# Side products of TensorE in four groups of 32 columns, and row maxima without a sum, in a two-layer graph attention kernel

## The chip, the cores and the metric

The kernel runs on one core of a Trainium2 chip. A core has TensorE (matrix products, into PSUM), VectorE, ScalarE, GpSimd and a synchronising engine that issues transfers; each runs its own list of instructions in order and waits for the others through semaphores. The metric is the device time of one execution in microseconds: 10420.47 us in the median of three runs of the kernel before (10419.83 to 10420.89).

## The reference

N = 3327 nodes with D = 128 features, and an adjacency matrix `adj` of zeros and ones with ones on its diagonal. Layer 0 is a graph attention, layer 1 eight "heads" of attention over a reshaped projection; each is added to its input and normalised by row.

```python
# layer 0
H = X @ W.T + b
s = H @ a_s
r = H @ a_r
e = leaky_relu(A * s + A * r.T, negative_slope=0.2)
att = softmax(where(A > 0, e, NEG), axis=1)
x = layernorm(x + att @ H)
# layer 1: h = 8, d = 128, n = 3327
q = (x @ Wq.T).reshape(d, n, h); k, v likewise
a = einsum('dnh,dmh->dnm', q, k) * d ** -0.5 + adj + adj
out = einsum('dnm,dmh->dnh', softmax(a, axis=2), v)
x = layernorm(x + out.reshape(n, h * d) @ Wo.T)
```

The reshape turns each of the 128 features into an attention of its own over all 3327 nodes with vectors of eight numbers. So layer 1 has 128 times 3327 x 3327 scores, each with an exponential, and this is nearly all of the work.

## The kernel before

**Main loop.** Features go in 32 groups of four. A group's columns go in 7 blocks of 476. The 3327 rows go in 26 tiles (`NT`), a "stretch" being three of them. A block has 26 rounds, and a round makes four score products (L135, one tile of scores `scb` for each two features, contraction over 32 rows, so that the four features use the four groups of 32 rows of TensorE's array) and then the four products with v of a tile of some rounds earlier (L800, `av`, one feature for each group of 32 columns of the array). Between them, a tile's scores take one of two ways. In a third of the tiles ScalarE makes the exponential from PSUM (L994) and GpSimd multiplies by a factor made of the adjacency (L995). In the others VectorE adds the adjacency from PSUM (L997) and ScalarE makes the exponential in place (L830). In the first two rounds of a stretch half the scores go one way and half the other; in the third all go VectorE's way. The PSUM tiles of ScalarE's way are one buffer, those of VectorE's way two, and the scores of a round wait for the buffer they write to be read. LAG = 4 is the number of rounds by which the products with v come later.

**Side work.** Layer 0 for tiles 1 to 25, the projections to q, k and v, and the last product with Wo are cut into small pieces and strewn over the rounds by `work_tensor` (pieces for TensorE, after the scores and ahead of the products with v) and `work` (pieces for VectorE and GpSimd, after the round's own additions). The function `lane` says which rounds have room for a piece: the middle one of each three, and the rounds at a block's ends. `finish_to` makes the pieces that are due before a group can start, one after the other. All of TensorE's pieces write to one PSUM bank, `bank`, which has one buffer. The order on every engine is that in which the program is written (`tc.manual_schedule`).

The pieces that matter here:

- `weigh` (L284) makes on VectorE, for a tile of 128 rows of layer 0 and one chunk of 128 columns, the maximum of a row `trow` (the same for all partitions) and a number of each partition, `er`. It asks also for the sum of what it makes, which is written to `spare` and read by nothing. The masks (`mask`, L295) are multiplied in on GpSimd. `count` (L304) is VectorE's count of zeros and ones in the adjacency.
- `product` (L311) multiplies 26 such chunks with `hsb` and sums them in the bank: 128 rows of weights, 128 columns, 129 numbers for each.
- `project` in `layer0` (L365) makes 128 columns of q, k or v from a tile of `x1T`; `halves` (L374, L377) or `values` (L396) empties the bank.
- `project` in `result` (L479) multiplies with Wo, eight pieces for a tile of 128 rows.

`load_row` (L257) brings `trow` from `td` in DRAM. The tile 0 of layer 0 is made ahead of the main loop, with `side=False`.

Of the kernel before, what the change touches and what calls it, by code (L numbers as in the profile page):

```python
# [8 lines left out]
F32 = mybir.dt.float32  # L9
# [4 lines left out]
ALU = mybir.AluOpType  # L14
# [3 lines left out]
P = 128  # L18
# [16 lines left out]
def _ap(t, offset, dims):  # L35
    return bass.AP(tensor=t.tensor, offset=t.offset + offset, ap=[list(d) for d in dims])
# [11 lines left out]
def kernel(  # L48
# [27 lines left out]
    nc = tc.nc  # L76
    N, D = x.shape
    H = wqT.shape[1]
    assert D == P
    NT = -(-N // P)  # L80
# [10 lines left out]
    FP = N // NT  # L91
    kr = [FP + (i < N - FP * NT) for i in range(NT)]
    assert FP == P - 1
    REST = N - FP * NT
# [7 lines left out]
    dram = ctx.enter_context(tc.tile_pool(name="dram", bufs=1, space=bass.MemoryType.DRAM))  # L102
# [6 lines left out]

    oT = dram.tile([H1, G], F32, name="oT")  # L110
    x1d = dram.tile([N, D], F32, name="x1d")
    td = dram.tile([1, N], F32, name="td")

# [12 lines left out]
    wo = const.tile([P, H, D], F32, name="wo")  # L128
# [15 lines left out]
    def special():  # L144
        with ExitStack() as sx, tc.manual_schedule(engines=ALL):
            keep = sx.enter_context(tc.tile_pool(name="sx_keep", bufs=1))
            bg2 = sx.enter_context(tc.tile_pool(name="sx_bg2", bufs=2))
            bga = sx.enter_context(tc.tile_pool(name="sx_bga", bufs=3))
            bgw = sx.enter_context(tc.tile_pool(name="sx_bgw", bufs=2))
            bg1 = sx.enter_context(tc.tile_pool(name="sx_bg1", bufs=1))  # L150
            bps = sx.enter_context(tc.tile_pool(name="sx_ps", bufs=1, space=bass.MemoryType.PSUM))

            CW = -(-NT // 3)
            CH = [(i, min(i + CW, NT)) for i in range(0, NT, CW)]

            wq = keep.tile([P, H * D], F32, name="wq")
# [13 lines left out]
            one_row = keep.tile([1, P], F32, name="one_row")  # L170
            nc.vector.memset(one_row, 1.0)
            nrm = keep.tile([1, 4], F32, name="nrm")

            spare = keep.tile([P, 1], F32, name="spare")
            ones = keep.tile([P, 1], F32, name="ones")
            nc.vector.memset(ones, 1.0)

            def bank(shape=(P, 512)):
                return bps.tile(list(shape), F32, tag="bank", name="bank")

            def rsqrt(s, v, r):

                def parts():
                    w = s["root"]
                    return w[:r, 0:1], w[:r, 1:2], w[:r, 2:3]

                def first():
                    s["root"] = bg1.tile([P, 4], F32, name="root")  # L190
                    nc.vector.tensor_scalar(parts()[0], v(), EPS, None, op0=ALU.add)

                def shift():
                    ve, y, z = parts()
                    nc.vector.tensor_scalar(z.bitcast(I32), ve.bitcast(I32), 1, None, op0=ALU.logical_shift_right)

                def guess():
                    ve, y, z = parts()
                    nc.vector.tensor_scalar(
                        y.bitcast(I32), z.bitcast(I32), -1.0, 1597463007.0, op0=ALU.mult, op1=ALU.add  # L200
                    )

                def error():
                    ve, y, z = parts()
                    nc.vector.tensor_scalar(z, y, ve, y, op0=ALU.mult, op1=ALU.mult)

                def factor():
                    ve, y, z = parts()
                    nc.vector.tensor_scalar(z, z, -0.5, 1.5, op0=ALU.mult, op1=ALU.add)

                def better():
                    ve, y, z = parts()
                    nc.vector.tensor_scalar(y, y, z, None, op0=ALU.mult)

                return [first, shift, guess] + [error, factor, better] * 3

            def together(*fs):
                def run():
# [22 lines left out]
            def layer0(t, side=True, trow=None, bank=bank):  # L241
# [4 lines left out]
                r = rows[t]  # L246
                s = {"a": {}, "w": {}}
# [5 lines left out]
                        nc.sync.dma_start(s["x"][p0:p1], x[t * P + p0 : t * P + p1, :])  # L253

                def load_row():
                    s["t"] = bg2.tile([P, P], F32, name="trow")
                    nc.sync.dma_start(s["t"][:, :r], _ap(td, t * P, [[0, P], [1, r]]))  # L257

                def load_adj(n):
                    i0, i1 = CH[n]  # L260
# [15 lines left out]
                def weigh(n, c0, c1):  # L276
                    i0 = CH[n][0]
                    if c0 == i0:
                        s["w"][n] = bgw.tile([P, CW, P], F32, name="w")
                    for i in range(c0, c1):  # L280
                        w, e = s["w"][n][:, i - i0, :r], er[:, i : i + 1]
                        if side:

                            nc.vector.tensor_scalar(  # L284
                                w, s["t"][:, :r], e, None, op0=ALU.max, op1=ALU.add, accum_out=spare[:, 0:1]
                            )
                        else:
                            nc.vector.scalar_tensor_tensor(
                                w, s["b"][:, :r], e, s["a"][n][:, i - i0, :r], op0=ALU.max, op1=ALU.mult
                            )  # L290
# [17 lines left out]
                def product(i):  # L308
                    if i == 0:
                        s["p"] = bank()  # L310
                    nc.tensor.matmul(  # L311
                        s["p"][:r, : D + 1],
                        s["w"][i // CW][: kr[i], i % CW, :r],
                        hsb[: kr[i], i, :],
                        start=(i == 0),
                        stop=(i == NT - 1),
                    )
# [43 lines left out]
                QW = 128 if side else 512  # L361

                def project(w, c):
                    s["b"] = bank()
                    nc.tensor.matmul(s["b"][:r, :QW], s["xT"][:, :r], w[:, c : c + QW], start=True, stop=True)  # L365

                def halves(dst, c, scale):
                    if c % 512 == 0:
# [53 lines left out]
                for n, (i0, i1) in enumerate(CH):  # L422

                    aside.append(("n", ("P", q0 + n - 2, 0)))
                    for c0 in range(i0, i1, 3):
                        c1 = min(c0 + 3, i1)
# [6 lines left out]
                    c = [("d", lambda n=n, h=h, k=k: count(n, h, k)) for h in range(3) for k in range(2)]  # L433
# [6 lines left out]
            def result(t):  # L440

                r = rows[t]
                s = {}
# [32 lines left out]
                def project(h):  # L476
                    if h == 0:
                        s["b"] = bank()
                    nc.tensor.matmul(  # L479
                        s["b"][:r, :D], s["ot"][:, h, :r], wo[:, h, :], start=(h == 0), stop=(h == H - 1)  # L480
                    )

                def finish():
# [32 lines left out]
            def judge():  # L516

                s = {}
                lim = 2.718281828 ** ((1 - ALPHA) * SAFE0)

                def load():
                    s["t"] = bg1.tile([P, NT], F32, name="jt")
                    nc.gpsimd.memset(s["t"], 1.0)
                    nc.sync.dma_start(s["t"][:FP, :], td[0, : FP * NT].rearrange("(p i) -> p i", i=NT))
                    nc.sync.dma_start(s["t"][FP:P, :REST], td[:, FP * NT :])

                def square(n, w, i):
                    u = bg1.tile([P, H, P], F32, name="ot")[:, :4, :].rearrange("p a b -> p (a b)")
# [73 lines left out]
            with ExitStack() as st:  # L602
# [6 lines left out]
                xT = pro.tile([P, P * NT], F32, name="xT")  # L609
# [39 lines left out]
                for b, (n0, _) in enumerate(blocks):  # L649
                    pr = pps.tile([P, 512], F32, tag="mm", name="pr")  # L650
                    nc.tensor.matmul(pr[:1, :WB], ascol, hT[:, n0 : n0 + WB], start=True, stop=True)
                    nc.scalar.activation(trs[b], pr[:1, :WB], AF.Exp, scale=ALPHA - 1.0)
                    nc.scalar.dma_start(td[:, n0 : n0 + WB], trs[b])

                for n, i0 in enumerate(range(0, NT, 3)):
                    pb = pps.tile([P, 512], F32, tag="mm", name="pb")[:, : 3 * (D + 1)].rearrange(
# [51 lines left out]
            for m, st_ in enumerate(stretch):  # L708
                starts[len(rounds)] = m
                if len(st_) > 1:  # L710
                    i = st_[0]
# [242 lines left out]
            for g in range(NG):  # L954
                k4, v4, _ = group
                for b in range(NBLK):
                    s = Block()
# [440 lines left out]
```

## Time and profile before

| what | value |
|---|---|
| time, median of 3 | 10420.47 us |
| span of the profiled execution | 10418.4 us |
| TensorE matmuls busy | 10195.1 us (98%) |
| ScalarE busy | 10088.8 us (97%) |
| VectorE busy | 9410.9 us (90%) |
| GpSimd busy | 9223.5 us (89%) |
| L311, matmul records and their busy time | 1300, 318.4 us |
| L365 (three groups) | 1200, 293.9 us |
| L479 | 416, 101.5 us |
| L284, maxima | 650 operations, with their accumulator readings 220.9 us |

The profile counts an engine as busy while an instruction of it is in work. Matmuls overlap and their ends are modelled, so that a busy TensorE is not one at its peak; there the distance from one start to the next says more than the length. An fp32 product is two records of a matmul and two of a weight load. "Idle before <-" tells how long an engine stood still before the instructions of a group and what released it. The chain that ended last is the way back from the last instruction through whatever released each one. Line numbers are those of the kernel before; in the kernel after, the products of L311 and L365 stand in the helpers `by_columns` (L224) and `whole` (L182), those of L479 in `by_columns` too.

### The profile page before, as it was taken

How to read it: one execution, taken by the hardware profiler on the slowest of the kernel's cores; microseconds unless marked ns; L12 is line 12 of the kernel's file. 1: busy time of each engine (PE TensorE's matmuls, PEld its weight loads, DVE VectorE, ACT ScalarE, POOL GpSimd, SP SyncE). 2: the span in 40 equal slices, each digit the busy share in tenths (PEclk: the TensorE clock that was granted, in tenths of full speed). 3: DMA queues.
4: the chain of work that ended last, by engine and by line, in shares of the span. 5: the costliest groups of instructions: out<-in, count | busy, mean ns of one | idle time of the engine just before them, and what ended most of it. 6: DMA issues, size and time to landing. Idle time of an engine off the chain costs nothing.

```text
span 10418.4 us, 195134 instructions
## 1 busy us (share of the span) xinstructions
PE 10195.1 (98%) x73245; PEld 3823.1 (37%) x73245; DVE 9410.9 (90%) x12247; ACT 10088.8 (97%) x8311; POOL 9223.5 (89%) x4395
## 2 busy tenths in 40 slices
PE   7999999999999999999999999999999999999998
PEld 3333333333333333333333333333333333333333
DVE  6999999999989999989999999999999899998887
ACT  6999999999999999999999999999999999999998
POOL 6988898889888899888898888888888888898887
PEclk8999999999999999999999999999999999999999
DMA  6655555555555555555555555555555555545554
GB/s 173 199 172 163 168 167 170 169 167 162 172 163 163 170 161 167 173 164 163 163 166 172 167 173 162 154 171 171 167 170 163 158 171 170 171 147 170 162 157 125
DMA packets 1176730, 1728.90 MB, mean 166 GB/s; under 512 B 121853, under 2 KB 1164382, under 8 KB 1171548
## 3 DMA queue, kind: packets, MB, share of 16 engines
q1 hardware_dynamic: 1174410, 1714.80, 55.5%
q8 instruction: 576, 9.44, 0.4%
q14 instruction: 383, 3.13, 0.1%
q10 hardware_dynamic: 1361, 1.53, 0.1%
HBM read 1611.92 MB, written 103.95 MB: 165 GB/s over the span
## 4 chain that ended last, share of the span: by engine, by line
PE 84%; ACT 8%; DVE 4%; issue 1%; DMA 1%; POOL 1%; SPq 0%; DVEq 0%; ACTq 0%; POOLq 0%
PE av L800 44%; PE scb L135 34%; ACT e L994 5%; ACT e L830 3%; PE bank L311 3%; DVE e L997 2%; PE bank L365 2%; POOL e L995 1%; PE bank L479 1%; DVE o L809 1%; DMA at<-in_adjT_dram 0%; PE bank L460 0%; DVE ot L469 0%; DMA k4b<-kT 0%; DVE lo L377 0%
## 5 line engine op out<-in xcount | busy, mean ns | idle before, releaser
L995 POOL TENSOR_TENSOR e<-e,at 128x952 f32<-128x952 f32 x4032 | 8966.3, 2234 | 1078.4 <-ACT e L994 903.2
L997 DVE TENSOR_TENSOR e<-scb,at 128x952 f32<-128x952 f32 (+1 forms) x7616 | 8417.6, 1144 | 857.5 <-PE scb L135 639.1
L830 ACT ACTIVATE e<-e 128x1904 f32<-128x1904 f32 (+2 forms) x4256 | 6875.3, 1621 | 17.5 <-DVE e L997 16.4
L800 PE MATMUL av<-e,v4b 128*32 128x476 f32 x46592 | 5905.4, 575 | 37.6 <-DVE o L809 30.7
L135 PE MATMUL scb<-q4b,k4b 32*128 32x476 f32 (+1 forms) x23296 | 4339.0, 592 | 124.5 <-ACT e L994 62.3
L135 PEld LDWEIGHTS scb<-q4b,k4b 32*128 32x128 f32 (+1 forms) x23296 | 2378.4, 296 | 4925.1 <-issue 1936.8
L994 ACT ACTIVATE e<-scb 128x952 f32<-128x952 f32 x4032 | 3871.4, 960 | 228.9 <-PE scb L135 133.7
L800 PEld LDWEIGHTS av<-e,v4b 128*32 128x32 f32 x46592 | 948.3, 108 | 1223.1 <-issue 770.1
L311 PE MATMUL bank<-hsb,w 128*128 128x129 f32 (+2 forms) x1300 | 318.4, 327 | 0.0
L311 PEld LDWEIGHTS bank<-hsb,w 128*128 128x128 f32 (+2 forms) x1300 | 193.7, 188 | 148.2 <-issue 147.8
L304 DVE TENSOR_SCALAR_CACHE_REDUCE dump<-a 128x384 bf16<-128x384 f32 (+2 forms) x468 | 247.3, 528 | 0.6
L284 DVE TENSOR_SCALAR_CACHE_REDUCE w<-trow,er 128x128 f32<-128x128 f32 (+1 forms) x650 | 220.9, 340 | 20.6 <-DMA trow<-td 12.6
L295 POOL TENSOR_TENSOR w<-w,a 128x384 f32<-128x384 f32 (+3 forms) x225 | 221.8, 986 | 0.1
L809 DVE COPY o<-av 128x476 f32<-128x476 f32 x224 | 145.9, 651 | 27.6 <-PE av L800 6.8
L377 DVE SCALAR_TENSOR_TENSOR lo<-bank,hi 128x128 fp32r<-128x128 f32 (+1 forms) x400 | 116.6, 291 | 13.8
L374 DVE TENSOR_SCALAR hi<-bank 128x128 fp32r<-128x128 f32 (+1 forms) x400 | 112.3, 281 | 0.0
L365 PE MATMUL bank<-wv,x1T 128*128 128x128 f32 (+1 forms) x400 | 98.5, 328 | 4.1 <-DVE vb L396 4.0
L479 PE MATMUL bank<-wo,ot 128*128 128x128 f32 (+1 forms) x416 | 101.5, 330 | 0.4 <-DVE ot L469 0.4
L365 PE MATMUL bank<-wk,x1T 128*128 128x128 f32 (+1 forms) x400 | 97.7, 326 | 3.7 <-DVE lo L377 2.5
L365 PE MATMUL bank<-wq,x1T 128*128 128x128 f32 (+1 forms) x400 | 97.7, 326 | 3.2 <-DVE lo L377 2.5
L479 PEld LDWEIGHTS bank<-wo,ot 128*128 128x128 f32 (+1 forms) x416 | 63.0, 193 | 46.1 <-issue 45.5
L365 PEld LDWEIGHTS bank<-wv,x1T 128*128 128x128 f32 (+1 forms) x400 | 60.0, 189 | 50.8 <-issue 40.4
(111 smaller groups left out, 820.1 us busy)
## 6 DMA issues: line engine op xcount, KB each, us to landing
at<-in_adjT_dram SPq DMA_DIRECT2D x1736, 476.0 KB
at<-ftd SPq DMA_DIRECT2D x1953, 238.0 KB
q4b<-qT SPq DMA_DIRECT2D x1788, 29.8 KB
k4b<-kT SPq DMA_DIRECT2D x126, 415.9 KB
at<-in_adjT_dram SPq DMA_DIRECT2D x217, 208.2 KB
at<-in_adjT_dram SPq DMA_DIRECT2D x56, 714.0 KB
a<-in_adjT_dram SPq DMA_DIRECT2D x50, 504.0 KB
ftd<-at SPq DMA_DIRECT2D x63, 238.0 KB
```

What stands on the lines that cost most here:

```text
L135: nc.tensor.matmul(dst, k4[32 * j : 32 * j + H4, i::NT], q4[32 * j : 32 * j + H4, :nb], start=True, stop=stop,)
L295: nc.gpsimd.tensor_tensor(w, w, s["a"][n][:, c0 - i0 : c1 - i0, :r], op=ALU.mult)
L304: nc.vector.tensor_scalar(z, a, float(k), None, op0=ALU.is_equal, op1=ALU.add, accum_out=even[:, t, at : at + 1])
L311: nc.tensor.matmul(s["p"][:r, : D + 1], s["w"][i // CW][: kr[i], i % CW, :r], hsb[: kr[i], i, :], start=(i == 0), stop=(i == NT - 1),)
L365: nc.tensor.matmul(s["b"][:r, :QW], s["xT"][:, :r], w[:, c : c + QW], start=True, stop=True)
L479: nc.tensor.matmul(s["b"][:r, :D], s["ot"][:, h, :r], wo[:, h, :], start=(h == 0), stop=(h == H - 1))
L800: nc.tensor.matmul(s.av[32 * j : 32 * j + 32, :], s.v4[:r, j, i * H1 : i * H1 + 32], e[:r, j, :], start=(s.left == NT - 1), stop=(s.left = ...
L809: nc.vector.tensor_copy(o4, s.av)
L830: nc.scalar.activation(e, e, AF.Exp, scale=2.0)
L994: nc.scalar.activation(eh, z[:r, :, :WB], AF.Exp, scale=2.0)
L995: nc.gpsimd.tensor_tensor(eh, eh, ah, op=ALU.mult)
L997: nc.vector.tensor_tensor(eh, z[:r, :, :WB], ah, op=ALU.add)
```

## The change

The first part concerns TensorE. The side pieces of L311, L365 and L479 were each one product over the whole array of 128 columns. They become four products of 32 columns each, every one to its own 32 partitions of the bank, which is the form of the products with v that come after them. The numbers computed are the same. The second part concerns `weigh`: the sum and `spare` are gone. The row is laid out as three pieces of 43 numbers with one empty place after each, and the result is written as one run of 129. For this the tile `w` has rows of 129 numbers, `td` is longer by two, and `load_row` brings 129 numbers of which the last is not used (the two past the end of `td` are written with ones).

```diff
-    td = dram.tile([1, N], F32, name="td")
+    td = dram.tile([1, NT * P + 1], F32, name="td")
...
+            T3 = P // 3 + 1
...
-            spare = keep.tile([P, 1], F32, name="spare")
...
+            def whole(dst, w, mov, r, **kw):
+                nc.tensor.matmul(dst[:r], w[:, :r], mov, **kw)
...
+            def by_columns(dst, w, mov, r, **kw):
+
+                for c0 in range(0, r, 32):
+                    c1 = min(c0 + 32, r)
+                    nc.tensor.matmul(dst[c0:c1], w[:, c0:c1], mov, **kw)
...
                 def load_row():
-                    s["t"] = bg2.tile([P, P], F32, name="trow")
-                    nc.sync.dma_start(s["t"][:, :r], _ap(td, t * P, [[0, P], [1, r]]))
+
+                    s["t"] = bg2.tile([P, 3, T3 + 1], F32, name="trow")
+                    nc.sync.dma_start(s["t"][:, :, :T3], _ap(td, t * P, [[0, P], [T3, 3], [1, T3]]))
...
-                        s["w"][n] = bgw.tile([P, CW, P], F32, name="w")
+                        s["w"][n] = bgw.tile([P, CW, 3 * T3], F32, name="w")
...
                         if side:
 
-                            nc.vector.tensor_scalar(
-                                w, s["t"][:, :r], e, None, op0=ALU.max, op1=ALU.add, accum_out=spare[:, 0:1]
-                            )
+                            w = s["w"][n][:, i - i0, :].rearrange("p (a b) -> p a b", b=T3)
+                            nc.vector.tensor_scalar(w, s["t"][:, :, :T3], e, None, op0=ALU.max)
...
-                    nc.tensor.matmul(
-                        s["p"][:r, : D + 1],
-                        s["w"][i // CW][: kr[i], i % CW, :r],
+                    (by_columns if side else whole)(
+                        s["p"][:, : D + 1],
+                        s["w"][i // CW][: kr[i], i % CW, :],
                         hsb[: kr[i], i, :],
+                        r,
...
-                    nc.tensor.matmul(s["b"][:r, :QW], s["xT"][:, :r], w[:, c : c + QW], start=True, stop=True)
+                    (by_columns if side else whole)(
+                        s["b"][:, :QW], s["xT"], w[:, c : c + QW], r, start=True, stop=True
+                    )
...
-                    nc.tensor.matmul(
-                        s["b"][:r, :D], s["ot"][:, h, :r], wo[:, h, :], start=(h == 0), stop=(h == H - 1)
+                    by_columns(
+                        s["b"][:, :D], s["ot"][:, h, :], wo[:, h, :], r, start=(h == 0), stop=(h == H - 1)
                     )
...
-                    nc.sync.dma_start(s["t"][FP:P, :REST], td[:, FP * NT :])
+                    nc.sync.dma_start(s["t"][FP:P, :REST], td[:, FP * NT : N])
...
+                nc.scalar.dma_start(td[:, N:], one_row[:, : NT * P + 1 - N])
```

## The prediction

> **What bounds the kernel now.** I read the busy shares first, then the chain that ended last, then the costliest groups, and then single stretches.
>
> ```profile
> PE 10195.1 (98%) x73245; PEld 3823.1 (37%) x73245; DVE 9410.9 (90%) x12247; ACT 10088.8 (97%) x8311; POOL 9223.5 (89%) x4395
> PE 84%; ACT 8%; DVE 4%; issue 1%; DMA 1%; POOL 1%; SPq 0%; DVEq 0%; ACTq 0%; POOLq 0%
> L284 DVE TENSOR_SCALAR_CACHE_REDUCE w<-trow,er 128x128 f32<-128x128 f32 (+1 forms) x650 | 220.9, 340 | 20.6 <-DMA trow<-td 12.6
> L311 PE MATMUL bank<-hsb,w 128*128 128x129 f32 (+2 forms) x1300 | 318.4, 327 | 0.0
> L365 PE MATMUL bank<-wv,x1T 128*128 128x128 f32 (+1 forms) x400 | 98.5, 328 | 4.1 <-DVE vb L396 4.0
> L479 PE MATMUL bank<-wo,ot 128*128 128x128 f32 (+1 forms) x416 | 101.5, 330 | 0.4 <-DVE ot L469 0.4
> ```
>
> TensorE and ScalarE are both nearly full, so a gain on one soon meets the other. The chain runs through TensorE for 84%; the reader should see that the side pieces (L311, L365, L479) are few beside 46592 products with v, but stand in that chain. Each product is two matmul records because fp32 is run as two. TensorE's instructions in one stretch of three rounds:
>
> ```profile
> 5000.10 0.60 PE L135 MATMUL scb<-q4b,k4b 32*128 32x476 f32 x4
> 5000.63 0.49 PE L311 MATMUL bank<-hsb,w 128*128 128x129 f32 x2
> 5001.05 1.00 PE L800 MATMUL av<-e,v4b 128*32 128x476 f32 x8
> 5001.98 0.60 PE L135 MATMUL scb<-q4b,k4b 32*128 32x476 f32 x4
> 5002.52 1.01 PE L800 MATMUL av<-e,v4b 128*32 128x476 f32 x8
> 5003.45 1.04 PE L135 MATMUL scb<-q4b,k4b 32*128 32x476 f32 x4
> 5004.42 1.00 PE L800 MATMUL av<-e,v4b 128*32 128x476 f32 x8
> 5005.36 0.60 PE L135 MATMUL scb<-q4b,k4b 32*128 32x476 f32 x4
> ```
>
> Start to start is what counts here. Scores to the next product take 0.53 us, products with v 0.93, and the side product 5000.63 to 5001.05 = 0.42. The third round's scores take 1.04 instead of 0.60: taken one by one, its second pair starts 0.445 us after the first, 53 ns after VectorE's addition (L997) that frees their PSUM tile. That addition itself had waited for TensorE:
>
> ```profile
> 5002.69 3.26 DVE L997 TENSOR_TENSOR e<-scb,at 128x952 f32<-128x952 f32 x3 [0.30 <-PE scb L135]
> ```
>
> So a loop of TensorE and VectorE sets 5.26 us, and the side product is inside it. Where there is none, ScalarE runs without a gap:
>
> ```profile
> 10221.19 1.79 ACT L830 ACTIVATE e<-e 128x1904 f32<-128x1904 f32 x1
> 10222.88 0.96 ACT L994 ACTIVATE e<-scb 128x952 f32<-128x952 f32 x1
> 10223.72 1.80 ACT L830 ACTIVATE e<-e 128x1904 f32<-128x1904 f32 x1
> 10225.44 0.97 ACT L994 ACTIVATE e<-scb 128x952 f32<-128x952 f32 x1
> 10226.30 1.78 ACT L830 ACTIVATE e<-e 128x1904 f32<-128x1904 f32 x1
> ```
>
> From 10221.19 to 10226.30 are 5.1 us for the same four exponentials; the median of all such stretches is 5.068 without a side product and 5.259 with one. Whole blocks of 26 rounds (without, and with nine):
>
> ```profile
> 10209.26:10253.52 44.26, 42.64 (x312) 14.97 (x313) 38.19 (x36) 44.26 (x38) 40.07 (x19) 1.00 0.51 153
> 1267.07:1313.38 46.31, 45.84 (x335) 17.31 (x332) 40.59 (x48) 44.89 (x38) 40.85 (x20) 1.00 0.56 171
> ```
>
> ScalarE (fourth number after the length) is busy 44.26 of 44.26 in the first, 44.89 of 46.31 in the second. The difference is 2.05 us for nine products, 0.228 each, though each occupies TensorE for 0.42: the rest hides under ScalarE already.
>
> [...] the four column groups of a product with v start within 20 ns, and their second set starts 0.425 us after the first. [...] 0.512 from the second set to the next scores, of which 0.397 is streaming. [...] the product's second load starts 108 ns after the first, its second matmul 108 ns after that. [...]
>
> **The side pieces, part by part.** Lines 311, 365 and 479 of the side work are 650 + 600 + 208 = 1458 products. Each becomes four of 32 columns in the mode of the products with v that follow.
>
> Now: first load 0.107, second load beside the first matmul, second matmul 0.107, then 0.096 until the next load may start: 0.418. Then the products with v pay a first load of 0.425 - 0.397 = 0.027 that nothing hides. Together 0.445. After: a first load of 0.027, two sets that stream [...](0.1075 each, by the measure that 476 columns take 0.397), and no change of mode behind them; the next loads lie beside the second set, as the products' second loads do now. That is 0.242. If the load of each following set were not hidden, 0.027 twice, 0.296. The saving is between 0.15 and 0.20 us; I take 0.20, because the second set of the products with v shows a hidden load, and keep 0.15 for the range.
>
> How much of it reaches the end? In the middle of a block a product costs 5.259 - 5.068 = 0.19 over ScalarE's floor. With 0.20 less, TensorE's loop is 5.06, level with ScalarE. Two waits are in between. The second scores of the third-kind round can't start before VectorE's addition of the round before ends, 1.885 us after that round's start, which is when they start now; but the first pair goes ahead by 0.2, the addition that waited 0.30 for it follows, and that one starts the loop again. VectorE must then be free: its side operation between the two additions may last up to about 0.6. The counting (L304) takes 0.47 + 0.08, two halves (L374, L377) 0.6, two maxima 2 x 0.38 = 0.76 now. So the maxima would have become the bound there, and the second part of the change matters only through this.
>
> A fit of the 223 blocks' times to the products in them gives 0.178 us for each of 998 in the middle rounds and 0.242 for each of 452 at a block's ends: 178 + 109 = 287 us, the most that products can give back; hence no less than about 10133. I count 0.17 of the 0.178 in the middle (two bounds that are level disturb each other): 170 us. At the ends half of the projections wait for VectorE to empty the one bank (at 1265.71 a product waits 0.45 for L377), so an earlier start is lost there; I count 0.12: 54 us. Sum 224 us.
>
> **The maxima.** The operation loses its sum and the reading of the accumulator (83 ns, 650 times; 262 ns from one start to that reading, 119 from the reading to the next maximum, so 381). A plain one with a pointer scalar takes 214 ns at one element (L213); 129 elements[...] add 134: 348, less the 83 ns by which successive operations overlap, 265. Saved 116 x 650 = 75 us of VectorE, almost all of it beside other work. By itself I give it 0: stretches with two maxima have a median of 5.265 and 5.260 against 5.257 to 5.260 with other side work. The source is three rows of 43 in rows of 44, the destination one run of 129[...]. Rows of the masking operation (L295) now start every 129 elements: at most a few ns in 225 operations. The row loads bring 384 pieces of 172 bytes for 128 of 512, 25 times, a stage ahead of use; one small store at the start goes on ScalarE's queue, under 1 us.
>
> Added waits: TensorE gets 45 more instructions that only wait, each 51 ns, for its own earlier work[...].
>
> **The rivals.**
> 1. ScalarE or VectorE takes over sooner: only 0.08 reaches the end per product: 1458 x 0.08 = 117, so 10303. For it: ScalarE has 0.19 us per stretch to give and TensorE's loop then stands on it. Against: stretches without a product do reach 5.068 with all its waits.
> 2. Instruction issue: a product is now 16 instructions for 4. [...] Against: two waiting instructions of TensorE are 111 ns apart with nothing between, and 125 with a load and a matmul between.
> 3. [...] 2.23 us multiplications fill GpSimd for 89%, so VectorE would wait about 1 us per pair in 325 places: +290 - 224 = about 10490, slower. [...]
> 4. Nothing gained: the four groups take as long as the one: 10420.
>
> **How the numbers follow.** The forecast 0.68, rival 1 0.15, rival 2 0.04, rival 3 0.08, no change 0.05. Time: 10420 - 224 = about 10196. Low end: all 287 us, 10135. High end: rival 1 with its spread, 10340. Outside are rivals 2 to 4, 0.17. Faster 0.83, same 0.05, slower 0.12.
>
> **What would show it.** Right: in the middle of a block a side product followed by products with v 0.24 to 0.30 us later, stretches with one at 5.07 to 5.10, ScalarE's idle time from 228.9 us for L994 down, blocks with nine products near 44.9; maxima at about 350 ns without an accumulator reading. Wrong: matmuls of the four groups that start in turn and not together, maxima whose lengths spread over 1 us or start late after GpSimd's operations (rival 3), gaps of TensorE that nothing explains (rival 2), VectorE's additions that start later after scores than now (rival 1).

## The result, and the profile after

The kernel after takes 10168.64 us (median of four executions, 10167.89 to 10170.51), the kernel before 10420.43 beside it: a ratio of 0.9759 with a 95% interval of 0.9744 to 0.9773, or 252 us less. The forecast was 10196 with a range of 10135 to 10340. It is 27 us above the result: the change saved 252 us where 224 were forecast.

The page of the kernel after: busy shares, the chain that ended last by engine, and three of the costliest groups (busy time and mean of one, then idle time ahead of them and what ended it). L1007 is L994 of before, L224 is `by_columns`, L295 the maxima.

```profile
PE 9930.1 (98%) x81993; PEld 3841.6 (38%) x81993; DVE 9374.0 (92%) x11597; ACT 9981.3 (98%) x8311; POOL 9215.6 (91%) x4395
PE 79%; ACT 10%; DVE 5%; POOL 2%; issue 2%; DMA 1%; SPq 0%; DVEq 0%; POOLq 0%; ACTq 0%
L1007 ACT ACTIVATE e<-scb 128x952 f32<-128x952 f32 x4032 | 3881.2, 963 | 88.0 <-PE scb L135 59.4
L224 PE MATMUL bank<-hsb,w 128*32 128x129 f32 (+1 forms) x5200 | 277.9, 285 | 0.0
L295 DVE TENSOR_SCALAR w<-trow,er 128x129 f32<-128x129 f32 x650 | 201.4, 339 | 13.1 <-DMA trow<-td 13.1
```

The busy shares tell nearly nothing: TensorE and ScalarE read 98% now and 98% and 97% before, though the span is 2.4% shorter. The busy time of the products with `hsb` fell from 318.4 to only 277.9 us, because the four groups lie over each other and each record is still 285 ns long. Two numbers do speak. ScalarE's idle time ahead of its exponentials from PSUM fell from 228.9 us, in this line of before,

```profile
L994 ACT ACTIVATE e<-scb 128x952 f32<-128x952 f32 x4032 | 3871.4, 960 | 228.9 <-PE scb L135 133.7
```

to 88.0, and the chain has less of TensorE (79% for 84%) and more of ScalarE (10% for 8%). The stretch itself, from a view of single instructions in order of time (start, length, engine, operation, count):

```profile
2389.14 0.60 PE L135 MATMUL scb<-q4b,k4b 32*128 32x476 f32 x4
2389.67 0.42 PE L224 MATMUL bank<-wo,ot 128*32 128x128 f32 x8
2389.91 0.98 PE L813 MATMUL av<-e,v4b 128*32 128x476 f32 x8
2390.83 0.79 PE L135 MATMUL scb<-q4b,k4b 32*128 32x476 f32 x4
2390.89 0.60 DVE L295 TENSOR_SCALAR w<-trow,er 128x129 f32<-128x129 f32 x2
2391.53 4.50 DVE L1010 TENSOR_TENSOR e<-scb,at 128x952 f32<-128x952 f32 x4
2391.55 1.01 PE L813 MATMUL av<-e,v4b 128*32 128x476 f32 x8
2392.48 0.84 PE L135 MATMUL scb<-q4b,k4b 32*128 32x476 f32 x4
2393.26 1.00 PE L813 MATMUL av<-e,v4b 128*32 128x476 f32 x8
2394.21 0.60 PE L135 MATMUL scb<-q4b,k4b 32*128 32x476 f32 x4
```

Side product to the next products with v: 2389.91 - 2389.67 = 0.24, for 0.42 before. One by one, the four groups of a set start within 20 ns. The loads of the second set start 26 ns after the first set's matmuls, and those of the products with v 2 ns after the second set's: both lie beside matmuls that run. The products with v gain too: their own second set starts 0.399 us after their first, for 0.424 before. The stretch runs from 2389.14 to 2394.21, 5.07 us; kinds of stretches with a product have medians of 5.066 to 5.073 (5.257 to 5.265 before), those without one have 5.068 in both kernels.

To see where the time came from, I took the distance from each round's scores to the next round's, in both traces, and summed the differences by the place of the round in its block, over all blocks:

| rounds of a block | products there | saved, us | for each product |
|---|---|---|---|
| 4 to 23 (the middle) | 998 | 155.9 | 0.156 |
| 3 | 153 | 25.6 | 0.167 |
| 24 | 150 | 57.6 | 0.384 |
| 25 | 149 | 12.3 | 0.083 |
| 3, 24 and 25 (the ends) | 452 | 95.5 | 0.211 |
| 0 to 2 | 0 | -1.5 | |

The sum is 250 us, and the first scores start 2.6 us earlier (at 85.3 us for 87.9). The time from the start of the last block to VectorE's last instruction is 70 us in both.

The row of round 24 holds something that isn't its own. Rounds 22, 23 and 24 are one stretch, and 156 blocks have a product in round 22. In 16 blocks with a product in round 22 and none in round 24, round 24 still fell from 1.903 to 1.720 us (medians). With a product in both it fell from 2.322 to 1.932. So a product in round 24 costs 2.322 - 1.903 = 0.42 before and 1.932 - 1.720 = 0.21 after, and saves about 0.21, not 0.384. The rest, some 27 us of the 57.6, is what the products of round 22 save. With it the middle saves about 183 us, 0.18 for each product, and the ends about 69 us, 0.15 for each. A fit of what each block saved to the products in it agrees: 0.19 and 0.15.

### The profile page after: what moved, and what is told of

It reads as the page before. It is cut to its first block, busy times and chain, and to the rows that moved or that the text cites. A ratio compares the mean times of both kernels' runs of the same rounds, so it can differ in the third digit from the quotient of the medians.

```text
span 10166.1 us, 212027 instructions
## 1 busy us (share of the span) xinstructions
PE 9930.1 (98%) x81993; PEld 3841.6 (38%) x81993; DVE 9374.0 (92%) x11597; ACT 9981.3 (98%) x8311; POOL 9215.6 (91%) x4395
## 4 chain that ended last, share of the span: by engine, by line
PE 79%; ACT 10%; DVE 5%; POOL 2%; issue 2%; DMA 1%; SPq 0%; DVEq 0%; POOLq 0%; ACTq 0%
PE av L813 41%; PE scb L135 33%; ACT e L1007 5%; ACT e L843 5%; PE bank L224 4%; DVE e L1010 3%; POOL e L1008 2%; DVE o L822 1%; DMA at<-in_adjT_dram 0%; PE bank L472 0%; DMA k4b<-kT 0%; DMA at<-ftd 0%; POOL at L803 0%; DVE lo L389 0%; DVE ot L481 0%
## 5 line engine op out<-in xcount | busy, mean ns | idle before, releaser
L843 ACT ACTIVATE e<-e 128x1904 f32<-128x1904 f32 (+2 forms) x4256 | 6885.4, 1624 | 14.7 <-DVE e L1010 14.3
L135 PEld LDWEIGHTS scb<-q4b,k4b 32*128 32x128 f32 (+1 forms) x23296 | 2518.9, 295 | 4796.6 <-issue 2640.6
L1007 ACT ACTIVATE e<-scb 128x952 f32<-128x952 f32 x4032 | 3881.2, 963 | 88.0 <-PE scb L135 59.4
L813 PEld LDWEIGHTS av<-e,v4b 128*32 128x32 f32 x46592 | 1058.7, 108 | 1066.5 <-issue 621.5
L224 PE MATMUL bank<-hsb,w 128*32 128x129 f32 (+1 forms) x5200 | 277.9, 285 | 0.0
L295 DVE TENSOR_SCALAR w<-trow,er 128x129 f32<-128x129 f32 x650 | 201.4, 339 | 13.1 <-DMA trow<-td 13.1
L304 POOL TENSOR_TENSOR w<-w,a 128x384 f32<-128x384 f32 (+3 forms) x225 | 207.0, 920 | 0.1
L224 PEld LDWEIGHTS bank<-hsb,w 128*32 128x32 f32 (+1 forms) x5200 | 102.4, 108 | 148.4 <-issue 148.4
L224 PE MATMUL bank<-wk,x1T 128*32 128x128 f32 x1600 | 85.2, 284 | 10.7 <-DVE lo L389 10.7
L224 PE MATMUL bank<-wq,x1T 128*32 128x128 f32 x1600 | 85.2, 284 | 9.0 <-DVE lo L389 9.0
L224 PE MATMUL bank<-wv,x1T 128*32 128x128 f32 x1600 | 85.4, 285 | 5.0 <-DVE vb L408 4.0
L224 PE MATMUL bank<-wo,ot 128*32 128x128 f32 (+1 forms) x1664 | 88.8, 290 | 0.4 <-DVE ot L481 0.4
L408 DVE COPY vb<-bank 128x128 f32<-128x128 f32 (+1 forms) x200 | 56.2, 281 | 3.5 <-PE bank L224 3.5
```

Of the source, the lines that this page charges most:

```text
L135: nc.tensor.matmul(dst, k4[32 * j : 32 * j + H4, i::NT], q4[32 * j : 32 * j + H4, :nb], start=True, stop=stop,)
L224: nc.tensor.matmul(dst[c0:c1], w[:, c0:c1], mov, **kw)
L295: nc.vector.tensor_scalar(w, s["t"][:, :, :T3], e, None, op0=ALU.max)
L304: nc.gpsimd.tensor_tensor(w, w, s["a"][n][:, c0 - i0 : c1 - i0, :r], op=ALU.mult)
L813: nc.tensor.matmul(s.av[32 * j : 32 * j + 32, :], s.v4[:r, j, i * H1 : i * H1 + 32], e[:r, j, :], start=(s.left == NT - 1), stop=(s.left = ...
L843: nc.scalar.activation(e, e, AF.Exp, scale=2.0)
```

## The experiments

Every edit is one of the kernel after; ratios are to the kernel before, with their 95% intervals.

### Which of the two parts did it

The first has the product in groups and the maxima of before (plain rows of 128, with a sum):

```diff
...
-    w = s["w"][n][:, i - i0, :].rearrange("p (a b) -> p a b", b=T3)
-    nc.vector.tensor_scalar(w, s["t"][:, :, :T3], e, None, op0=ALU.max)
+    nc.vector.tensor_scalar(
+        w, s["t"][:, :r], e, None, op0=ALU.max, op1=ALU.add, accum_out=spare[:, 0:1]
+    )
```

> The products by four groups of 32 columns, with the maxima of before (sum and accumulator reading, rows of 128). Theory (the gain is TensorE's time in the loop, the maxima matter only where two of them stand between two additions): about 15 us over the kernel after, 10183 us (10172 to 10200); stretches of three rounds with one maximum or other side work at 5.07, with two maxima about 5.15. Rival (the second part carries a good share of the 252 us): 10290 us.

The second has the maxima of after and one product over the whole array:

```diff
 def by_columns(dst, w, mov, r, **kw):
-    for c0 in range(0, r, 32):
-        c1 = min(c0 + 32, r)
-        nc.tensor.matmul(dst[c0:c1], w[:, c0:c1], mov, **kw)
+    whole(dst, w, mov, r, **kw)
```

> The maxima of after, with every side product over the whole array as before. Theory: VectorE's 75 us lie beside TensorE's loop, so 10405 to 10421 us; stretches with a product stay at 5.26. Rival (VectorE's time reaches the end): about 10345 us.

Measured: the groups alone 10171.01 us, 0.976 (0.9746 to 0.9773), no different from the kernel after; the maxima alone 10419.83 us, 0.9999 (0.9991 to 1.0007), with stretches of 5.26. So the first part carries all of it, and the second is worth nothing that these runs resolve, with the first or without. I had expected 10183 us for the groups alone, and 5.15 for stretches with two maxima. The kernel with the groups and the old maxima shows why the sum costs nothing. VectorE's instructions in one of its stretches:

```profile
2389.30 0.34 DVE L295 TENSOR_SCALAR_CACHE_REDUCE w<-trow,er 128x128 f32<-128x128 f32 x1
2389.56 0.08 DVE L295 DVE_READ_ACCUMULATOR w<-trow,er 128x1 f32 x1
2389.68 0.35 DVE L295 TENSOR_SCALAR_CACHE_REDUCE w<-trow,er 128x128 f32<-128x128 f32 x1
2389.95 0.08 DVE L295 DVE_READ_ACCUMULATOR w<-trow,er 128x1 f32 x1
2389.95 4.50 DVE L1012 TENSOR_TENSOR e<-scb,at 128x952 f32<-128x952 f32 x4
```

The last accumulator reading (2389.95) lies beside the addition that starts at the same time, so two maxima take 2389.95 - 2389.30 = 0.65 us of VectorE between additions and not 0.76. Stretches with two such maxima have medians of 5.064 to 5.068 here, as good as with the new ones.

### What the rows of 43 are for

Two kernels take the sum away but not in the way of the change. The first keeps plain rows of 128:

```diff
-    s["t"] = bg2.tile([P, 3, T3 + 1], F32, name="trow")
-    nc.sync.dma_start(s["t"][:, :, :T3], _ap(td, t * P, [[0, P], [T3, 3], [1, T3]]))
+    s["t"] = bg2.tile([P, P], F32, name="trow")
+    nc.sync.dma_start(s["t"][:, :r], _ap(td, t * P, [[0, P], [1, r]]))
...
-    nc.vector.tensor_scalar(w, s["t"][:, :, :T3], e, None, op0=ALU.max)
+    nc.vector.tensor_scalar(w, s["t"][:, :r], e, None, op0=ALU.max)
```

> The kernel after, but the maxima without a sum read and write plain rows of 128[...]. Theory[...]: maxima start late or take 1 us and more, and VectorE's next addition is late in some 325 places: about 10455 us (10250 to 10700). Rival (no exclusion shows[...]): [...] 10166 us or a few less.

The second keeps 129 elements but puts them in one run, so that source and destination have the same odd count:

```diff
-    s["t"] = bg2.tile([P, 3, T3 + 1], F32, name="trow")
-    nc.sync.dma_start(s["t"][:, :, :T3], _ap(td, t * P, [[0, P], [T3, 3], [1, T3]]))
+    s["t"] = bg2.tile([P, 3, T3], F32, name="trow")
+    nc.sync.dma_start(s["t"].rearrange("p a b -> p (a b)"), _ap(td, t * P, [[0, P], [1, 3 * T3]]))
```

> The kernel after, but the maxima read one run of 129 numbers where after reads three rows of 43 with gaps; they write one run of 129 as after. Both counts are then odd and equal. Theory[...]: maxima of some 280 ns and up to 2.4 us, as on plain rows of 128, and 10600 to 10700 us. Rival ([...] the rows of 43 were not needed): 339 ns each and 10168 us.

Measured: 10676.77 us, 1.0248 (1.0234 to 1.0262), and 10678.92 us, 1.0245 (1.0228 to 1.0262): both 0.5 ms above the kernel after. The maxima in a view of one tile, with count, shortest, median and longest in ns; the kernel with rows of 128 first:

```profile
L294 DVE TENSOR_SCALAR w<-trow,er x650: 271/601/2368, 100.4 to 9544.5; 128x128 f32<-128x128 f32 x156, 128x127 f32<-128x127 f32 x7
```

and that with a run of 129:

```profile
L295 DVE TENSOR_SCALAR w<-trow,er x650: 269/605/2374, 102.4 to 9554.8; 128x129 f32<-128x129 f32 x163
```

In the kernel after, the same view gives 336, 339 and 348. The shortest are faster than the change's, by some 70 ns; the longest last as long as one of GpSimd's multiplications (2.23 us). One by one, a maximum that began at 2316.52 ended 0.08 us after GpSimd's operation had ended, and the one behind it took 274 ns. So on these rows a maximum can be quick, and can also last until an operation of GpSimd is over; with the rows of 43 all 650 take 336 to 348 ns and do neither. What makes the difference inside the engines, no run shows. The mean rises from 339 to 1022 ns, so 650 x 0.683 = 444 us of VectorE, and 508 us of time.

The time is more than the waits. Two lines of TensorE's, from the kernel with rows of 128:

```profile
2020.65 0.60 PE L135 MATMUL scb<-q4b,k4b 32*128 32x476 f32 x2 [2.51 <-DVE e L1009]
2023.35 1.81 PE L812 MATMUL av<-e,v4b 128*32 128x476 f32 x8
```

TensorE stands still for 2.51 us until a late addition ends, and a little later eight matmuls with v take 1.81 us and not 1.0. Between 2021.97 and 2025.38 its granted clock is 0.50. In the main loop of this kernel such pieces at half the clock add up to 594 us in 109 pieces, against 20 us in four in the kernel after; each of the 109 begins within 4 us after a gap of more than 0.5 us on TensorE. These gaps themselves add up to 299 us for 34. So the waits of TensorE are some 265 us more, close to the 290 that the prediction gave this rival, and the half clock costs up to (594 - 20) / 2 = 287 us more. The second figure is an estimate and an upper one; the share of each in the 508 us was not measured apart.

So the rows with gaps don't make a maximum quicker. They are what makes it harmless to leave the sum out: 336 to 348 ns for each, where the maxima with a sum took 333 to 351 on plain rows in the kernel before.

### Why four groups are quick: the number of groups, and the form

```diff
-    for c0 in range(0, r, 32):
-        c1 = min(c0 + 32, r)
+    for c0 in range(0, r, 64):
+        c1 = min(c0 + 64, r)
```

> The kernel after, but the side products by two groups of 64 columns, a form that is not that of the products with v. Theory A (the change of form ahead of the products with v, and the load that can't be hidden across it, is what is saved): 0.053 + 2 x 0.1075 + 0.096 = 0.36 us to the next product with v and an open load behind it, so about 0.05 saved of 0.445 and some 10345 us. Theory B (smaller loads and groups side by side are what counts): 0.27 us, and about 10185 us.

Measured: 10357.16 us, 0.9938 (0.9924 to 0.9951), so a quarter of the gain. Three lines of TensorE's:

```profile
2007.25 0.60 PE L135 MATMUL scb<-q4b,k4b 32*128 32x476 f32 x4
2007.79 0.44 PE L224 MATMUL bank<-wk,x1T 128*64 128x128 f32 x4
2008.16 1.00 PE L813 MATMUL av<-e,v4b 128*32 128x476 f32 x8
```

The product now takes 2008.16 - 2007.79 = 0.37. One by one, both groups start together and their second set 0.160 us later, but the load of the products with v starts 0.207 us after that set: it is not taken in beside it. With 32 columns, the form of what follows, it is. Stretches have a median of 5.208, 0.05 below before for 0.05 in the product. Between the two forms lie 0.370 - 0.243 = 0.127 us (medians). Of these 0.10 are the wait behind the last set (0.210 to the products with v, 0.110 with 32 columns) and 0.03 the larger first load; one load more, 0.025, lies open inside the products with v (0.423 to their second set, for 0.399). So smaller loads are the smaller part; having the same form as the next work is the larger. Before the change, with one group of 128 columns, the wait behind the last set was 0.205, as with two groups.

### The price of one product, by doubling it

Layer 0's products and the projections of tiles 1 to 25 (1250 products) are made twice in groups; Wo's stay single. For layer 0 numerator and sum both come twice.

```diff
...
-    (by_columns if side else whole)(
-        s["b"][:, :QW], s["xT"], w[:, c : c + QW], r, start=True, stop=True
-    )
+    for _ in range(2 if side else 1):
+        (by_columns if side else whole)(
+            s["b"][:, :QW], s["xT"], w[:, c : c + QW], r, start=True, stop=True
+        )
```

> The kernel after, with every product of layer 0's sums and of the projections to q, k and v made twice in the form of four groups (the sums then count each product twice in numerator and denominator; the products with Wo stay single). Theory (after the change TensorE's loop with one product is level with ScalarE's 5.068 us, so a second one of 0.215 us shows in full in the middle, and by about 0.15 at a block's ends): 856 x 0.2 + 387 x 0.15 = about 230 more, 10396 us, stretches with such products at 5.27 us. Rival (ScalarE alone is the bound and TensorE has room below it): under 10230 us.

Measured: 10408.6 us, 0.9988 (0.9981 to 0.9995), 240 us above the kernel after: 240 / 1250 = 0.192 for each product that was added. From the first of two products to the products with v it is 0.461 us, for 0.243 with one, so the second adds 0.218. Stretches with a doubled product have medians of about 5.28, those with a single one 5.07. The change took some 0.2 us of TensorE out of a stretch and the stretch lost 0.19; here 0.218 are put back and it gains 0.21. It is TensorE's time that counts there.

### Is ScalarE the floor of 5.07?

The prediction said so. This kernel, which no longer computes the whole reference, leaves the last eighth of the columns out of the exponential in place (L843), some 0.42 us of ScalarE's work in a stretch by estimate (1.59 us for 1.79 in the traces, twice in a stretch):

```diff
-    e = s.e[i][: kr[i], h0:h1, :]
+    e = s.e[i][: kr[i], h0:h1, : WB - WB // 8]
```

> The kernel after, with the last eighth of the columns left out of ScalarE's exponentials in place (L830 before, L843 after): 416 of 476 columns, so that ScalarE has about 0.42 us less to do in three rounds. Theory (ScalarE's 5.068 us is the floor after the change, and TensorE's loop stands at 5.055 with a product and 4.84 without): stretches without a product near 4.85, those with one near 5.05, about 145 us less in all, 10020 us (9980 to 10080). Rival 1 (GpSimd or VectorE, both over 90% busy, are as near): 10140 to 10168 us. Rival 2 (TensorE's loop is far below ScalarE's floor): under 9900 us.

Measured: 10160.19 us, 0.9749 (0.9733 to 0.9765): the same as the kernel after within the intervals, where the theory had 10020. Stretches stay at 5.06 to 5.07, with and without a product. Two lines of its page:

```profile
PE 9904.3 (98%) x81993; PEld 3818.6 (38%) x81993; DVE 9370.7 (92%) x11597; ACT 9418.8 (93%) x8311; POOL 9206.3 (91%) x4395
L1007 ACT ACTIVATE e<-scb 128x952 f32<-128x952 f32 x4032 | 3877.3, 962 | 637.2 <-PE scb L135 589.5
```

ScalarE's busy time fell by 563 us and its idle time ahead of L1007 rose from 88 to 637: all that was saved became waiting for scores. A stretch without a product shows for what:

```profile
4999.48 3.47 DVE L1010 TENSOR_TENSOR e<-scb,at 128x952 f32<-128x952 f32 x3
5000.10 0.96 ACT L1007 ACTIVATE e<-scb 128x952 f32<-128x952 f32 x1 [0.36 <-PE scb L135]
5000.97 1.59 ACT L843 ACTIVATE e<-e 128x1668 f32<-128x1668 f32 x1
5001.12 0.60 PE L135 MATMUL scb<-q4b,k4b 32*128 32x476 f32 x4
5002.59 1.02 PE L135 MATMUL scb<-q4b,k4b 32*128 32x476 f32 x4
5004.47 0.81 PE L135 MATMUL scb<-q4b,k4b 32*128 32x476 f32 x4
5005.17 0.96 ACT L1007 ACTIVATE e<-scb 128x952 f32<-128x952 f32 x1 [0.28 <-PE scb L135]
5006.19 0.60 PE L135 MATMUL scb<-q4b,k4b 32*128 32x476 f32 x4
```

It is a loop through the PSUM buffers. The first round's scores are followed by L1007, which empties ScalarE's single buffer at 5001.06; the second round's scores start 0.06 later, 1.72 after the first round's (5006.19 - 5004.47). Those scores feed an addition of VectorE, the third of the first line, which ends at 4999.48 + 3.47 = 5002.95 and frees the buffer that the third round's second pair of scores waits for: one by one, it starts 1.888 us after 5001.12, 0.06 after that end. From there come 0.525 to the products with v and 0.94 to the next first round: 1.717 + 1.888 + 0.525 + 0.94 = 5.07. Neither a side product nor L843 is in this loop. Its length happens to equal ScalarE's own work (5.064 for the four exponentials back to back) and the loop of TensorE and VectorE that the prediction found for a stretch with a product, less the 0.20 of the groups (5.259 - 0.20 = 5.06).

### Opening that loop

In the second round of a stretch the two halves change places, so that the half for VectorE's addition comes first and ScalarE's half second:

```diff
-    rounds += [[(i, 1), (i + 1, 0)], [(i, 0), (i + 1, 1)]]
+    rounds += [[(i, 1), (i + 1, 0)], [(i + 1, 1), (i, 0)]]
```

> The kernel after, but in the second round of each stretch the scores of VectorE's way are made ahead of those of ScalarE's way, whose one PSUM buffer is still being read. Theory (5.07 us is held twice: by ScalarE's own work of 5.06, and by a loop over the PSUM tiles, first round's scores to L1007 to the buffer free 1.717, second round's scores to VectorE's addition to the next first round 3.353): the swap opens only the loop, ScalarE stays, so 10168 us within 15. Rival (the PSUM loop alone holds it): about 100 us less.

The same with the shorter exponential of the last experiment (again without the last eighth of the columns):

> The same swap, with the last eighth of the columns left out of ScalarE's exponentials in place, as in the run with fewer exponentials (10160 us). Theory (both holds are taken away here, and TensorE's loop of 4.87 us without a product and 5.055 to 5.07 with one remains): stretches without a product near 4.87, with one near 5.06, 570 x 0.2 = about 115 us less than that run, 10045 us (10000 to 10100). Rival (something else holds 5.07, such as GpSimd): 10140 to 10170 us.

Measured: the swap alone 10159.47 us, 0.9749 (0.9736 to 0.9762); with the shorter exponential 10130.31 us, 0.9722 (0.9707 to 0.9737). The swap alone can't be told from the kernel after. Both edits together are 38 us below the kernel after, where each alone gives 8 to 9: the loop and ScalarE bind at the same length, and one shows only once the other is gone. That the swap opens the loop shows in its trace: 72 of 366 stretches without a product (those that start in rounds 7 to 19) take less than 4.9 us, and none in the kernel after, though the whole gains nothing as long as ScalarE has its full work. But I had expected some 115 us below the shorter exponential, and it is 30, with intervals that just touch. Stretches with a product stay at 5.06, as the loop of TensorE and VectorE has it; those without one fall to about 5.0 in the mean, not to 4.87. Of the same 366, 111 are below 4.9, and others stay near 5.0 or at 5.2. What holds those was not found.

### The ends of the blocks

A product in round 24 still costs 0.21 us in the kernel after, where one in the middle costs nothing. The place for it is taken away:

```diff
-    return int(middle or n == 3 or n >= NR - 2)
+    return int(middle or n == 3 or n == NR - 1)
```

> The kernel after, but TensorE's side pieces get no room in the last but one round of a block (n = 24), where a piece still lengthens the round by about 0.2 us; they move to middle rounds, three in ten of which are empty and where a piece now costs nothing. Theory: about 150 pieces x 0.2 = 25 to 30 us less, some 10140 us. Rival (pieces come later, and the ones made one after the other ahead of a group grow): no gain, or slower by some 10 us.

Measured: 10181.2 us, 0.9769 (0.9753 to 0.9785). Rounds 24 and 25 are another 59 us below the kernel after, and the mean of the blocks (leaving out the few above 46.5 us) goes from 44.69 to 44.44 us. But the time is 13 us longer, as the rival had it. Of the 150 products 126 find another place, 96 of them in the middle. The others come too late: 32 products are made after the last block's scores instead of 8, and from the start of the last block to the end it takes 133 us instead of 70; the sixth block, at whose end products that are due are made one after the other (10 for 6), takes 58.0 instead of 52.9. To tell whether the end suffers from places missing in the last groups or all along, the place is taken away only in the groups between the first and the last three:

```diff
 def work_tensor(now, n):
+    if n == NR - 2 and total <= now < (NG - 3) * total:
+        return
```

> The kernel after, without TensorE's side piece at n = 24 in groups 1 to 28, but with it in the first group and the last three, so that pieces are less late there. Theory (the losses of the run with nine places lie in the block ahead of the second group and after the last block): about 10130 to 10150 us. Rival (the places are missing in the middle groups too, and the pieces left over are as many): 10175 us or more.

and in another kernel it is moved to round 2 of each block:

```diff
-    return int(middle or n == 3 or n >= NR - 2)
+    return int(middle or n in (2, 3) or n == NR - 1)
```

> The kernel after, but TensorE's side piece of the last but one round of a block (n = 24, where it costs about 0.2 us) is made in the third (n = 2) instead, so that a block has ten places as before. In the run with nine places the blocks took 44.44 us in the mean for 44.69, but left-over pieces made the end 64 us longer and a block ahead of the second group 5. Theory: the same gain in the blocks, without the losses: about 10125 us (10110 to 10150). Rival (a piece at n = 2 costs as much as at n = 24): 10168 us.

Measured: 10173.81 us, 0.9763 (0.975 to 0.9777), with 32 products after the last block's scores and an end of 127 us still: the places are missing all along. With round 2 instead 10136.98 us (10135.01 to 10140.39), 0.9728 (0.9715 to 0.9742): 31.7 us below the kernel after, with the whole of the reference computed. Round 24 falls from 1.933 us with a product to 1.720 without, and round 2, with a product in 168 blocks, goes only from 2.080 to 2.097, so most of a product is hidden there; by what, was not looked into. The end takes 86 us. This is the fastest kernel of the study that leaves nothing out; with the swap it was not tried.

## Why the prediction came out right, and where it did not

**The size of one product: right.** 0.242 was worked out, 0.243 measured one by one (median), with both hidden loads that the forecast took from the products with v. The 0.397 us that it took for 476 columns agree with the trace of before, where the 14 matmul records of L646, 476 columns each, mostly start 0.399 us apart. The first set of groups (four starts within 20 ns), the hidden second load (26 ns behind the first matmuls' start) and the missing change of form (0.110 us behind the last set, for 0.205) each show in the trace, and the kernel with two groups shows that the last is the larger part.

**The middle of a block: right, a little low.** 0.17 for each of 998 were 170 us; about 183 came, 0.18 each. The stretches reach 5.07 as said. So the two bounds that are level disturb each other less than the discount allowed.

**The ends: the term that was mis-sized most.** 0.12 for each of 452 were 54 us; about 69 came, 0.15 each. The step that failed is "half of the projections wait for VectorE to empty the one bank [...], so an earlier start is lost there", taken for all the ends. In the trace it holds in round 25 alone. There 44 products for q and k start 1.04 us after the second pair of scores, for 0.75 before, and 21 for v 0.62 for 0.53: 44 x 0.29 + 21 x 0.10 = 15 us are lost, 0.03 for each of the 452 and not 0.08. In rounds 3 and 24 no product waits for the bank in either kernel.

**The added waits: given nothing, and worth a little.** The prediction had TensorE's 45 waiting instructions wait for its own earlier work and put no price on them. All 45 stand in round 25, where the product waits for the bank, and each begins 39 ns after VectorE has emptied it, so nothing hides them: from the end of VectorE's piece to the first matmul of a product for q or k it is 146 ns, for 54 before. That is 44 x 0.092 = 4 us, a part of the 15.

Together the terms miss by +13 in the middle, +15 at the ends, -1.5 in the first rounds and +2 ahead of the first block, which is the 28 us between 252 and 224.

**Readings that were off.** The 46592 are matmul records of the products with v, so 23296 products; the 23296 scores, in fp32r, are one record each. The fit of 0.178 and 0.242 is loose: done again on the trace of before, it gives 0.16 and 0.15 over all blocks, and 0.12 and 0.24 without the blocks above 46.5 us. The forecast for the ends was right not to lean on 0.242.

**The floor: the number was right, its name was not.** "ScalarE's floor" of 5.068 is also the length of a loop of PSUM buffers through L1007 and VectorE's addition, and shortening ScalarE's work alone changed nothing. ScalarE without a gap in a stretch, which the prediction took as proof, is what an equal loop looks like too. The forecast needed only the number, which the stretches without a product gave.

**The maxima.** Given 0, and worth 0. The step "two maxima 2 x 0.38 = 0.76 now. So the maxima would have become the bound there" failed: they take 0.65 and fit. The 348 ns worked out for one are 339, with 3 rows of 43 into a run of 129, and none is stretched by GpSimd: the longest takes 348. (The 134 ns for 129 elements are an estimate, from the trace of before: L304 takes 543 ns for 384 columns and 409 for 256, so 134 for 128.) That rows of 43 keep the maxima clear of GpSimd's operations was not shown by that trace; the kernels with plain rows and with one run of 129 show it. The rival in which VectorE waits for those operations was the right fear with too small a price: where it was made to happen it cost 508 us, not 290. Its price had the waits and left out TensorE's lower clock behind them (0.50, at most 287 us by the estimate above). That the masking operation would cost "at most a few ns" more had the wrong sign: it is quicker, as told below.

**The rivals.** ScalarE or VectorE taking over with 0.08 per product, and no gain at all, are ruled out by 252 us. Instruction issue is ruled out by a stretch that holds 44 matmuls and 44 loads in 5.07 us.

**What would show it.** Products 0.24 to 0.30 us ahead of those with v (0.24), stretches at 5.07 to 5.10 (5.066 to 5.073), ScalarE's idle time down (228.9 to 88.0), blocks with nine products near 44.9 (44.74 in the mean of 61), maxima near 350 ns without a reading (339): all came, and none of the signs of the rivals.

## What to carry to other kernels

A small product between larger ones can cost as much in loads and changes of form around it as in its own streaming (here, by the prediction's estimate, 0.23 and 0.215 of 0.445 us): give it the groups of the work that follows, and count from one start to the next, since the busy share hardly moves. An engine without gaps in a stretch need not be all that sets it; a loop through the buffers may have the same length (here 5.07 us, beside ScalarE's 5.064), and only taking away each of the two, and then both, tells. Before a reduction nobody reads is taken from an operation in SBUF, ask whether the operation without it still keeps clear of GpSimd's (here a maximum on plain rows took 333 to 351 ns with the sum, and 271 to 2368 without). When savings are summed by place, cut where a loop ends: a cut through a stretch gave round 24 what round 22 had saved.

## What the runs showed of the hardware that was not expected

- GpSimd's masking operation, most often on 3 x 128 columns, got quicker when its rows started every 129 floats and not every 128: a mean of 920 ns for 986 over 225 operations. Only the pitch is common to the kernels that show it: with the maxima of before, with the maxima that wait for GpSimd and without the groups it is 915 to 920 too.
- The reading of VectorE's accumulator, 83 ns long, lies beside the operation behind it, so that the second of two such readings costs nothing.
- TensorE's clock was granted at half for a few us after gaps of 0.8 to 4.6 us (median 2.1), though not after every gap: 109 pieces, 594 us in all, in the main loop of the kernel with rows of 128. In such a piece the second set of a product with v starts 0.794 us after the first, for 0.42.
- A maximum from one run of 129 into another took 269 to 2374 ns, much as on plain rows of 128 (271 to 2368); from 3 rows of 43 into a run of 129 it took 336 to 348.
